# Projections of the second relational layer made inside the first, two accumulators for gathered blocks, and GIN's residual on TensorE

## The chip, the cores and the metric

One Trainium2 chip, one of its cores. Each time is the device time of one execution in microseconds (us); the number that counts is the median of the runs.

## The reference, cut to what matters

A graph of 3125 nodes with 128 features and 100000 edges, sorted by destination, goes through four parts, each followed by a residual and a layer norm: three GCN layers, one sum of neighbours, a GIN layer with two batch norms, and two relational layers. The change touches the end of the third part and the whole fourth:

```
h = relu(batchnorm(h @ W2 + b2))                      # end of GIN
x = layernorm(x + h)

def rgcn_layer(x, src, dst, etype, W, W_root, b, num_rels):      # 8 relations
    h = einsum('ni,rio->rno', x, W)
    msg = h[etype, src]
    seg = dst * num_rels + etype
    mean = segment_sum(msg, seg) / maximum(segment_sum(1, seg), 1)
    return mean.reshape(N, num_rels, do).sum(axis=1) + x @ W_root + b

h = relu(rgcn_layer(x, src, dst, edge_type, W1, root1, b1, 8))   # 128 -> 256
x = layernorm(x + rgcn_layer(h, src, dst, edge_type, W2, root2, b2, 8))   # 256 -> 128
```

## The kernel before, in words

The nodes are cut into 25 blocks of 128, and the blocks into chunks of four or three, `CH = ((0, 4), (4, 3), (7, 4), (11, 3), (14, 4), (18, 3), (21, 4))`. From the edge list the kernel builds count matrices in memory first: one over all edges (`adj`, `adj_t`) for the first three parts, and one for each relation (`rel`, 8-bit counts) for the destinations of blocks 0 to 13. The destinations of blocks 14 to 24 get no relation matrix; there the rows of the sources are gathered edge by edge. The dense part and the gathered part of a relational layer run side by side.

GIN ends with a loop over `CH` (L661 to L667): the transposed result `y2` is turned back by TensorE into a PSUM tile, DVE adds the residual to `xa`, and `normalise` (L118) makes the layer norm: statistics of each block on DVE, a square root on ACT, a reciprocal and the scaling of each block on DVE.

The relational layers hold float32 rows in several pieces, so that fast matmuls keep the precision. `split2` (L691) makes a pair of float32r pieces (the tile `hilo`). `store3` (L697) makes three bf16 pieces by copy on ACT, subtraction on DVE, copy on ACT, subtraction on DVE, with the tiles `t3` (shown as t) and `e3` (shown as e) of two buffers each, and stores them to a table in memory by a DMA on SP's queue: `xt_d` for layer 1's input, `ht_d` for layer 2's, one table of 3200 rows for each relation.

`relation` (L712) makes one product of a chunk of destinations with the rows of all 25 source blocks, for one relation. In each of five groups it loads 8-bit counts of five source blocks (`m8`, six buffers, on SP), casts them to float32r (`m`, three buffers; DVE for groups 0, 2, 4 at L728, ACT for 1 and 3 at L726), and multiplies with both pieces into the PSUM tile `acc` (L731, three buffers). After each group it advances `work` by a rate of 2.2 steps.

`work` is the generator `gathered` (L742). A step gathers 128 edges' rows from the table by an indirect DMA of GpSimd (`gx`, L765, twelve buffers), and adds them by three bf16 matmuls with a one-hot tile `oh` (made on DVE, L757) into `ga` (L773), a PSUM tile of 128 x 1024, one buffer, for one destination block and all relations. At the end of a block `put1` (L820) or `put2` (L893) evicts it.

In layer 1 the loop L827 takes the four dense chunks, for each the eight relations, with the means in `z` (L832); `linear1` (L796) then multiplies `z` by the eight matrices W1 and adds the root term, starting with the root term (L806), then L808, in float32, and ACT writes `hT` (L810), the transposed hidden rows. For the gathered chunks `put1` calls `linear1`. All of linear1's PSUM tiles are of the tag `mi`, two buffers.

Layer 2 begins with the root term `oT` (L872). `project` (L842) then makes h W2 for one relation after the other, for each block two float32 matmuls of 128 columns (L848), four or three blocks a PSUM tile, and each tile goes through `store3`. Relation 7 is made last, and its pieces are also split straight from PSUM, since layer 2 begins with it; the other relations' rows come back from memory by `fetch` (L854: load, two additions, split). The loop L906 takes for each relation the four dense chunks, scales (L913) and adds (L915); the gathers for layer 2 need the whole table. `finish` makes the last layer norm.

The order of instructions on each engine is fixed before the run by a scheduler: it takes the program's order as priority, and lets a later instruction go first where, by its own model of times, the earlier one is not ready. At run time each engine and each queue keeps to that order. The recording counts each float32 matmul as two instructions.

Of the kernel before, what the change touches and what calls it, by code (L numbers as in the profile page):

```python
# [21 lines left out]
P = 128  # L22
D = 128
# [22 lines left out]
def cols(m0, nb):  # L46
    return slice(m0 * P, (m0 + nb) * P)
# [25 lines left out]
def listed(ctx: ExitStack, tc: tile.TileContext, p: dict, out: bass.AP, bad):  # L73
# [43 lines left out]

    def normalise(y, v, nb):  # L118

        st = small.tile([P, 4, 6], F32, name="st")  # L120
        mv = small.tile([P, 4, 2], F32, name="mv")
        for i in range(nb):
            nc.vector.bn_stats(st[:, i, :], v[:, i, :])
            nc.vector.bn_aggr(mv[:, i, :], st[:, i, :])
        rs = small.tile([P, 4], F32, name="rs")
        nc.scalar.activation(rs[:, :nb], mv[:, :nb, 1], AF.Sqrt, bias=eps_ln, scale=1.0)
        nc.vector.reciprocal(rs[:, :nb], rs[:, :nb])
        for i in range(nb):
            nc.vector.tensor_scalar(
                y[:, i, :], v[:, i, :], mv[:, i, 0:1], rs[:, i : i + 1],  # L130
                op0=OP.subtract, op1=OP.mult,
            )
# [4 lines left out]
    def blocks(ap):  # L137
        return ap.rearrange("p (b c) -> p b c", c=P)

    with tc.tile_pool(name="f_bg", bufs=1) as bg, tc.tile_pool(  # L140
# [322 lines left out]
        with tc.tile_pool(name="f_nd", bufs=1) as nd:  # L463
# [209 lines left out]
    with tc.tile_pool(name="f_rel", bufs=1) as rp, tc.tile_pool(  # L673
# [17 lines left out]
        def split2(pieces, m0, nb, x):  # L691

            hi, lo = [t[:, m0 : m0 + nb, :] for t in pieces]
            nc.scalar.copy(hi, x)
            nc.vector.tensor_sub(lo, x, hi.bitcast(F32))  # L695

        def store3(table, row0, m0, nb, x):  # L697

            t = rp.tile([P, 4, 3, D], BF, name="t3", bufs=2)
            a, b, c = [t[:, :nb, i, :] for i in range(3)]  # L700
            e = rp.tile([P, 4, D], F32, name="e3", bufs=2)[:, :nb, :]
            nc.scalar.copy(a, x)  # L702
            nc.vector.tensor_sub(e, x, a)  # L703
            nc.scalar.copy(b, e)  # L704
            nc.vector.tensor_sub(c, e, b)  # L705
            r0 = row0 + m0 * P
            nc.sync.dma_start(table[r0 : r0 + nb * P].rearrange("(b p) c -> p b c", p=P),
                              t[:, :nb].rearrange("p b i c -> p b (i c)"))

        ahead = [0.0]  # L710

        def relation(r, m0, nb, pieces, work, rate):  # L712

            acc = psum.tile([P, 512], F32, name="acc", tag="acc", bufs=3)
            w = nb * P
            for g in range(5):
# [12 lines left out]
                for k in range(5):  # L729
                    for i, x in enumerate(pieces):  # L730
                        nc.tensor.matmul(  # L731
                            acc[:, :w], x[:, 5 * g + k, :],
                            m[:, k].rearrange("p b d -> p (b d)")[:, :w],
                            start=(g == 0 and k == 0 and i == 0), stop=(g == 4 and k == 4 and i == 1),
                        )
# [6 lines left out]
        def gathered(table, rows, put):  # L742


            for g in range(NG):
# [37 lines left out]
        with tc.tile_pool(name="f_z", bufs=1) as zp:  # L783
            w1 = zp.tile([P, R, O1], F32, name="w1")
            nc.scalar.dma_start(w1, p["L3_gnn_W1"].rearrange("r i o -> i r o"))
            root1 = zp.tile([P, O1], F32, name="root1")
            nc.scalar.dma_start(root1, p["L3_gnn_root1"])
# [5 lines left out]
            for m0, nb in CH:  # L793
                store3(xt_d, 0, m0, nb, x3[:, m0 : m0 + nb, :])

            def linear1(z, m0, nb):  # L796
# [40 lines left out]
        with tc.tile_pool(name="f_hr", bufs=1) as hp:  # L837
            wr = hp.tile([P, 2, R, D], F32, name="wr", tag="wr")
            for a in range(2):
                nc.scalar.dma_start(wr[:, a], p["L3_gnn_W2"][:, a * P : (a + 1) * P, :].rearrange("r i o -> i r o"))  # L840

            def project(r, pieces):  # L842

                for m0, nb in CH:
                    o = psum.tile([P, 512], F32, name="mi", tag="mi", bufs=2)
                    for i in range(nb):
                        for a in range(2):
                            nc.tensor.matmul(o[:, cols(i, 1)], hT[:, a, cols(m0 + i, 1)], wr[:, a, r, :],  # L848
                                             start=(a == 0), stop=(a == 1))
                    store3(ht_d, r * NP, m0, nb, blocks(o[:, : nb * P]))  # L850
                    if pieces is not None:
                        split2(pieces, m0, nb, blocks(o[:, : nb * P]))

            def fetch(r):  # L854
# [14 lines left out]
            for m0, nb in CH:  # L869
# [21 lines left out]
            def put2(b, wn, acc, inv):  # L891
                s = hp.tile([P, P * R], F32, name="sg", tag="wr")
                nc.vector.tensor_mul(s[:, : wn * R], acc, inv)  # L893
# [10 lines left out]
            ahead[0] = -14  # L904
            order = [R - 1] + list(range(R - 1))
            for n, r in enumerate(order):  # L906
                nxt = None
                for i, (m0, nb) in enumerate(DENSE):
# [6 lines left out]
                    nc.vector.tensor_add(oT[:, c], oT[:, c], s[:, :w])  # L915
                    if i == 0 and n + 1 < R:
                        nxt = fetch(order[n + 1])
                    if n == R - 1:
                        finish(m0, nb)
# [620 lines left out]
```

## Time and profile before

| | us |
|---|---|
| median of 3 runs | 2266.65 |
| lowest, highest | 2266.39, 2271.27 |
| the profiled execution, its own time | 2383.56 |
| its span, first to last instruction | 2381.7 |

In the profiled execution TensorE's mean granted clock is 0.919, and the engines are busy for these shares of the span: TensorE 84%, its weight loads 60%, VectorE 62%, ScalarE 33%, GpSimd 38%. They are means over stages with different limits, so the stages have to be looked at one by one. A group in the profile is named by its line, its engine, its operation and by the tile written and the tiles read (`out<-in`). PE is TensorE, PEld its weight loads, DVE VectorE, ACT ScalarE, POOL GpSimd, and SP the engine whose queue issues most DMAs; SPq and ACTq are the queues. A busy TensorE is not a TensorE at its peak, since matmuls overlap in their pipeline and their ends are modelled.

### The profile page before, as it was taken

The page shows a single profiled execution, that of the slowest core. Times are in us where ns is not written, and L with a number is a line of the kernel's source. Part 1 is how long each engine was busy: PE and PEld are TensorE (multiplying, and loading weights), DVE is VectorE, ACT ScalarE, POOL GpSimd, SP SyncE. Part 2 cuts the span into 40 slices and gives each one's busy share as a digit, 9 for nine tenths or more (in the row PEclk, how much of TensorE's full clock was granted, in tenths as well). Part 3 has the DMA queues.
Part 4 walks back from the last instruction along what each step waited for, and adds up shares of the span by engine and source line. Part 5 has one row for each costly group of instructions (what it writes and reads, how often), then busy time and mean ns, then how long its engine had stood idle before and what let it go on. Part 6 is the DMA issues. An engine that isn't in the chain of part 4 may idle for free. (4 is left out here: it accounts for less than half of the span.)

```text
span 2381.7 us, 33681 instructions
## 1 busy us (share of the span) xinstructions
PE 1990.4 (84%) x13076; PEld 1424.5 (60%) x13076; DVE 1473.2 (62%) x2403; ACT 789.9 (33%) x1027; POOL 896.3 (38%) x898
## 2 busy tenths in 40 slices
PE   2676679999999999578989999888776798898785
PEld 1454446666655555256676775775675676776674
DVE  5888879999984310656443562441445677786764
ACT  1676725545431100422221221221343332322320
POOL 3222021212110000036575563772003577776665
PEclk9777789999999999689989999998998999998997
DMA  3444477888886665256465663662545677777662
GB/s 89 180 181 180 185 185 240 286 280 269 277 278 189 198 171 152 91 150 183 133 167 142 167 185 92 172 180 62 164 136 164 174 232 205 221 229 207 167 195 76
DMA packets 381459, 430.71 MB, mean 181 GB/s; under 512 B 28747, under 2 KB 347117, under 8 KB 381288
## 3 DMA queue, kind: packets, MB, share of 16 engines
q1 hardware_dynamic: 311134, 276.49, 38.4%
q0 software_dynamic: 45920, 119.66, 16.5%
q10 hardware_dynamic: 24234, 32.31, 4.5%
q8 instruction: 104, 1.70, 0.3%
q14 instruction: 67, 0.55, 0.1%
HBM read 316.76 MB, written 111.58 MB: 180 GB/s over the span
## 5 line engine op out<-in xcount | busy, mean ns | idle before, releaser
L731 PE MATMUL acc<-m,hilo 128*128 128x384 f32 (+1 forms) x3200 | 774.2, 386 | 56.2 <-issue 39.2
L731 PEld LDWEIGHTS acc<-m,hilo 128*128 128x128 f32 x3200 | 584.0, 196 | 137.9 <-issue 60.1
L765 POOL DMA_INDIRECT gx<-xt_d,gsrc x355 | 361.8, 1019 | 573.4 <-DMA m<-rel 339.8
L531 PE MATMUL acc<-m,parts 128*128 128x512 bf16 (+1 forms) x2625 | 539.0, 357 | 15.0 <-issue 12.8
L728 DVE CAST m<-m 128x2560 fp32r<-128x2560 uint8 (+1 forms) x192 | 401.8, 2097 | 231.5 <-ACT m L726 64.9
L765 POOL DMA_INDIRECT gx<-ht_d,gsrc x355 | 387.2, 1091 | 346.6 <-issue 265.9
L726 ACT CAST m<-m 128x1920 fp32r<-128x1920 uint8 (+1 forms) x128 | 264.2, 2064 | 622.5 <-PE ga L773 188.8
L531 PEld LDWEIGHTS <-parts 128*128 128x128 bf16 x2625 | 255.2, 98 | 237.4 <-issue 17.7
L773 PE MATMUL ga<-oh,gx 128*128 128x192 bf16 (+1 forms) x2442 | 265.7, 248 | 107.1 <-DVE sg L893 25.7
L773 PEld LDWEIGHTS <-gx 128*128 128x128 bf16 x2442 | 180.8, 100 | 194.0 <-issue 139.4
L448 ACT CAST rb<-bld 128x800 uint16<-128x800 f32 x179 | 143.9, 828 | 129.8 <-PE bld L441 121.6
L757 DVE TENSOR_TENSOR oh<-iota,gkey 128x768 bf16<-128x768 bf16 (+1 forms) x188 | 99.2, 530 | 133.8 <-PE ga L773 75.5
L455 POOL DMA_DIRECT2D rel<-rb x112 | 64.3, 582 | 287.5 <-ACT rb L448 162.7
L848 PE MATMUL mi<-wr,hT 128*128 128x128 f32 x800 | 107.2, 294 | 34.9 <-DVE e L703 33.8
L848 PEld LDWEIGHTS mi<-wr,hT 128*128 128x128 f32 x800 | 100.4, 205 | 42.7 <-DVE e L703 40.0
L154 DVE TENSOR_TENSOR lo<-iota,kT 128x2048 bf16<-128x2048 bf16 x100 | 122.0, 1220 | 0.8 <-PE bld L264 0.8
L441 PE MATMUL bld<-rhq,rlo 128*128 128x200 bf16 x896 | 107.7, 252 | 1.8 <-DVE rb L450 1.1
L264 PE MATMUL bld<-hi,lo 128*128 128x50 bf16 x1600 | 74.3, 200 | 39.9 <-DVE hi L154 24.5
L441 PEld LDWEIGHTS <-rlo 128*128 128x128 bf16 x896 | 82.5, 98 | 36.7 <-issue 9.1
L154 DVE TENSOR_TENSOR rhq<-iota,kT 128x3200 bf16<-128x3200 bf16 x56 | 102.2, 1824 | 0.0
L264 PEld LDWEIGHTS <-lo 128*128 128x128 bf16 x1600 | 63.5, 107 | 64.3 <-DVE hi L154 27.3
L276 PE MATMUL mi<-identb,at 128*128 128x128 bf16 x625 | 66.3, 272 | 34.0 <-ACT at L266 20.4
(211 smaller groups left out, 1801.4 us busy)
## 6 DMA issues: line engine op xcount, KB each, us to landing
m<-rel SPq DMA_DIRECT2D x160, 320.0 KB
rel<-rb POOLq DMA_DIRECT2D x112, 400.0 KB
m<-adj SPq DMA_DIRECT2D x60, 640.0 KB
m<-rel SPq DMA_DIRECT2D x160, 240.0 KB
m<-adj_t SPq DMA_DIRECT2D x40, 640.0 KB
m<-adj SPq DMA_DIRECT2D x45, 480.0 KB
adj_t<-at SPq DMA_DIRECT2D x25, 800.0 KB
adj<-av SPq DMA_DIRECT2D x25, 800.0 KB
```

Source lines behind the costliest of these rows:

```text
L154: nc.vector.tensor_tensor(o, (iota2 if of is None else of)[:, None, :width, :].to_broadcast([P, PU // 2, width, 2]), k[:, :, None, :].to_b ...
L264: nc.tensor.matmul(pt[:, j, : 2 * NB], lo[:, j // 2, :, j % 2], hi[:, j // 2, :, j % 2], start=True, stop=True)
L441: nc.tensor.matmul(pt[:, k, : R * NB], lo[:, j // 2, :, j % 2], hq[:, j // 2, :, j % 2], start=True, stop=True)
L448: nc.scalar.copy(o, src)
L531: nc.tensor.matmul(o, x[:, k, :], m(k - k0), start=(k == 0 and i == 0), stop=last and more is None)
L726: nc.scalar.copy(v, src)
L728: nc.vector.tensor_copy(v, src)
L731: nc.tensor.matmul(acc[:, :w], x[:, 5 * g + k, :], m[:, k].rearrange("p b d -> p (b d)")[:, :w], start=(g == 0 and k == 0 and i == 0), sto ...
L757: nc.vector.tensor_tensor(oh[:, : nt // 2], iota2[:, None, : GW * R, :].to_broadcast([P, nt // 2, GW * R, 2]), gkey[:, g, t : t + nt].rear ...
L765: nc.gpsimd.indirect_dma_start(out=gx.rearrange("p i c -> p (i c)"), out_offset=None, in_=table[:], in_offset=bass.IndirectOffsetOnAxis(ap ...
L773: nc.tensor.matmul(acc[:, a:z], gx[:, i, :], oh[:, t % 4 // 2, a - c0 : z - c0, t % 2], start=(a // 512 not in seen), stop=(t == GT[g] - 1 ...
L848: nc.tensor.matmul(o[:, cols(i, 1)], hT[:, a, cols(m0 + i, 1)], wr[:, a, r, :], start=(a == 0), stop=(a == 1))
```

## The change

- The projections h W2 move into `linear1`: as soon as a chunk of `hT` is written, two PSUM tiles of 512 columns are made for each of its blocks, each with four relations side by side (two float32 matmuls of 512 columns instead of eight of 128), and each goes through `store3`. `W2` is loaded at the beginning of layer 1. Layer 2 takes the relations in order from 0, and all of them through `fetch`.
- In `linear1` the root term is the last of the nine matmuls and no longer the first.
- `ga` gets two buffers, `acc` two instead of three. The tile of `put2` (sg) gets its own place.
- The rows of the cast tile `m` are 520 elements apart and no longer 512.
- In GIN's last loop two float32 matmuls of each block, one with `y2` and one with the identity and `xa`, add the residual in PSUM, in the tag `bld`; the norm reads PSUM, and every second block of it is scaled by ACT.

```diff
+    def normalise(y, v, nb, shared=False):
...
+        if shared:
+            ng = small.tile([P, 4], F32, name="ng")
+            nc.vector.scalar_tensor_tensor(ng[:, :nb], mv[:, :nb, 0], -1.0, rs[:, :nb],
+                                           op0=OP.mult, op1=OP.mult)
         for i in range(nb):
+            if shared and i % 2 == 0:
+                nc.scalar.activation(y[:, i, :], v[:, i, :], AF.Identity, bias=ng[:, i : i + 1],
+                                     scale=rs[:, i : i + 1])
+                continue
             nc.vector.tensor_scalar(
...
             for m0, nb in CH:
-                t = psum.tile([P, 512], F32, name="mi", tag="mi", bufs=2)
+                t = psum.tile([P, 512], F32, name="bld", tag="bld", bufs=2)
                 for i in range(nb):
-                    nc.tensor.transpose(t[:, cols(i, 1)], y2[:, cols(m0 + i, 1)], ident)
-                xs = xa[:, m0 : m0 + nb, :]
-                nc.vector.tensor_add(xs, blocks(t[:, : nb * P]), xs)
-                normalise(xs, xs, nb)
+                    o = t[:, cols(i, 1)]
+                    nc.tensor.matmul(o, y2[:, cols(m0 + i, 1)], ident, start=True, stop=False)
+                    nc.tensor.matmul(o, ident, xa[:, m0 + i, :], start=False, stop=True)
+                normalise(xa[:, m0 : m0 + nb, :], blocks(t), nb, True)
...
-            acc = psum.tile([P, 512], F32, name="acc", tag="acc", bufs=3)
+            acc = psum.tile([P, 512], F32, name="acc", tag="acc", bufs=2)
...
-                m = rp.tile([P, 5, 4, P], F32R, name="m", bufs=3)
-                v = m[:, :, :nb, :]
+                m = rp.tile([P, 5, 4 * P + 8], F32R, name="m", bufs=3)
+                v = m[:, :, :w].rearrange("p k (b d) -> p k b d", d=P)
...
-                acc = psum.tile([P, P * R], F32, name="ga", tag="ga", bufs=1)
+                acc = psum.tile([P, P * R], F32, name="ga", tag="ga", bufs=2)
...
+            wr = zp.tile([P, 2, R, D], F32, name="wr")
+            for a in range(2):
+                nc.scalar.dma_start(wr[:, a], p["L3_gnn_W2"][:, a * P : (a + 1) * P, :].rearrange("r i o -> i r o"))
...
-                    nc.tensor.matmul(o[:, :w], root1[:, c], x3t[:, :w], start=True, stop=False)
                     for r in range(R):
                         nc.tensor.matmul(o[:, :w], w1[:, r, c], z[:, r, :w],
-                                         start=False, stop=(r == R - 1))
+                                         start=(r == 0), stop=False)
+                    nc.tensor.matmul(o[:, :w], root1[:, c], x3t[:, :w], start=False, stop=True)
...
+                for b in range(m0, m0 + nb):
+                    for r in range(0, R, 4):
+                        o = psum.tile([P, 512], F32, name="mi", tag="mi", bufs=2)
+                        for a in range(2):
+                            nc.tensor.matmul(o, hT[:, a, cols(b, 1)],
+                                             wr[:, a, r : r + 4, :].rearrange("p r c -> p (r c)"),
+                                             start=(a == 0), stop=(a == 1))
+                        store3(ht_d.rearrange("(r n) c -> n r c", r=R)[b * P : (b + 1) * P, r : r + 4],
+                               blocks(o))
...
-            def project(r, pieces):
...
-            hr = pair()
-            for r in range(R):
-                project(r, hr if r == R - 1 else None)
...
-            order = [R - 1] + list(range(R - 1))
-            for n, r in enumerate(order):
+            hr = fetch(0)
+            for r in range(R):
```

More of the change, by code (lines that the diff above doesn't have):

```diff
@@ L115, in listed @@
     gsrc = [const.tile([P, NG, GM], I32, name=f"gsrc{i}") for i in range(2)]
-    def normalise(y, v, nb):
+    def normalise(y, v, nb, shared=False):
         st = small.tile([P, 4, 6], F32, name="st")
@@ L695, in split2, with store3 @@
             nc.vector.tensor_sub(lo, x, hi.bitcast(F32))
-        def store3(table, row0, m0, nb, x):
+        def store3(rows, x):
+            n = x.shape[1]
             t = rp.tile([P, 4, 3, D], BF, name="t3", bufs=2)
-            a, b, c = [t[:, :nb, i, :] for i in range(3)]
-            e = rp.tile([P, 4, D], F32, name="e3", bufs=2)[:, :nb, :]
+            a, b, c = [t[:, :n, i, :] for i in range(3)]
+            e = rp.tile([P, 4, D], F32, name="e3", bufs=2)[:, :n, :]
             nc.scalar.copy(a, x)
@@ L705, in store3 @@
             nc.vector.tensor_sub(c, e, b)
-            r0 = row0 + m0 * P
-            nc.sync.dma_start(table[r0 : r0 + nb * P].rearrange("(b p) c -> p b c", p=P),
-                              t[:, :nb].rearrange("p b i c -> p b (i c)"))
+            nc.sync.dma_start(rows, t[:, :n].rearrange("p b i c -> p b (i c)"))
         ahead = [0.0]
         def relation(r, m0, nb, pieces, work, rate):
-            acc = psum.tile([P, 512], F32, name="acc", tag="acc", bufs=3)
+            acc = psum.tile([P, 512], F32, name="acc", tag="acc", bufs=2)
             w = nb * P
@@ L732, in relation @@
                             acc[:, :w], x[:, 5 * g + k, :],
-                            m[:, k].rearrange("p b d -> p (b d)")[:, :w],
+                            m[:, k, :w],
                             start=(g == 0 and k == 0 and i == 0), stop=(g == 4 and k == 4 and i == 1),
@@ L793, in listed @@
             for m0, nb in CH:
-                store3(xt_d, 0, m0, nb, x3[:, m0 : m0 + nb, :])
+                store3(xt_d[m0 * P : (m0 + nb) * P].rearrange("(b p) c -> p b c", p=P),
+                       x3[:, m0 : m0 + nb, :])
             def linear1(z, m0, nb):
@@ L837, in listed @@
         with tc.tile_pool(name="f_hr", bufs=1) as hp:
-            wr = hp.tile([P, 2, R, D], F32, name="wr", tag="wr")
-            for a in range(2):
-                nc.scalar.dma_start(wr[:, a], p["L3_gnn_W2"][:, a * P : (a + 1) * P, :].rearrange("r i o -> i r o"))
-            def project(r, pieces):
[L844 to L852, printed above, removed]
             def fetch(r):
@@ L891, in put2 @@
             def put2(b, wn, acc, inv):
-                s = hp.tile([P, P * R], F32, name="sg", tag="wr")
+                s = hp.tile([P, P * R], F32, name="sg", bufs=1)
                 nc.vector.tensor_mul(s[:, : wn * R], acc, inv)
@@ L915, in listed @@
                     nc.vector.tensor_add(oT[:, c], oT[:, c], s[:, :w])
-                    if i == 0 and n + 1 < R:
-                        nxt = fetch(order[n + 1])
-                    if n == R - 1:
+                    if i == 0 and r + 1 < R:
+                        nxt = fetch(r + 1)
+                    if r == R - 1:
                         finish(m0, nb)
```

## The prediction

> **What bounds the kernel now.** I first looked for where the edited lines run (the views of single lines): the first relational layer's products (L731, tile acc) run from 1022 us, its last linear1 (L808) ends at 1652, the projections (L848) lie between 1662 and 1811, and from 1818 the second layer runs alone. Cut at those points, the table of stages reads (us, then busy us of each engine, TensorE's clock, the DMA share, GB/s):
>
> ```profile
> core 0: us, PE busy (x) PEld busy (x) DVE busy (x) ACT busy (x) POOL busy (x), PEclk, DMA share, GB/s
> 955.00:1022.00 67.00, 36.09 (x114) 20.85 (x111) 45.80 (x133) 33.64 (x54) 0.00 (x0) 0.72 0.36 110
> 1022.00:1605.00 583.00, 512.66 (x2887) 400.75 (x2887) 270.92 (x227) 137.60 (x81) 343.40 (x336) 0.93 0.57 156
> 1605.00:1652.00 47.00, 38.05 (x155) 21.90 (x156) 6.94 (x11) 3.17 (x6) 18.42 (x20) 0.85 0.24 68
> 1652.00:1818.00 166.00, 129.22 (x877) 113.91 (x876) 81.84 (x129) 71.67 (x130) 0.00 (x0) 0.95 0.43 141
> 1818.00:2382.00 564.00, 459.16 (x2798) 374.62 (x2797) 383.15 (x467) 151.96 (x102) 387.16 (x355) 0.91 0.66 190
> ```
>
> Layer 1 is TensorE's: 513 of 583 us, DVE under half, ACT a quarter. Between the layers stand 166 us in which GpSimd does nothing and no engine is full. In layer 2 TensorE has 459 of 564 us, DVE 383. So the first question is what times the 166 us. The chain of waits inside them, then who waited there:
>
> ```profile
> by line: DMA ht_d<-t 32.0%; DVE e L703 11.9%; DVE t L705 11.1%; PE mi L848 11.0%; ACT t L702 9.2%; ACT t L704 8.9%; PE mi L872 6.5%; issue 4.7%; DVE hilo L695 2.2%; PE acc L731 2.0%; DVE m L728 0.7%; ACTq L702 0.5%; DVEq L705 0.0%
> ...
> DVE e L703 <- ACT t L702: 70.3, 36, 27.2
> ACT t L702 <- DMA ht_d<-t: 46.0, 33, 4.2
> ...
> PE mi L848 <- DVE e L703: 33.8, 28, 2.7
> ```
>
> Not the matmuls (11%) but the splitting chain store3 sets the pace: copy, subtract, copy, subtract, store, and the copy of the next-but-one chunk waits until the store has landed (32% of the chain), since t3 has two buffers. 56 stores leave between 1666.9 and 1815.9: 149/55 = 2.71 us each.
>
> TensorE's own waits, 1022 to 1605 and then 1818 to 2344 (total us, times, longest), show the single accumulator of the gathered blocks: at a block's end the next block's matmuls wait for the eviction.
>
> ```profile
> PE ga L773 <- DVE z L820: 24.0, 6, 6.8
> PE acc L731 <- issue: 19.2, 26, 2.2
> ...
> PE ga L773 <- DVE sg L893: 25.7, 6, 7.9
> ...
> PE acc L731 <- DVE m L728: 11.2, 5, 5.4
> ```
>
> Last, the casts of the 8-bit relation blocks on DVE by shape (count, busy us, mean ns):
>
> ```profile
> L728 DVE CAST m<-m 128x2560 fp32r<-128x2560 uint8 x96 | 269.7, 2813 | 98.8 <-remote 45.7 <-issue 22.2 <-PE ga L773 15.8
> L728 DVE CAST m<-m 128x1920 fp32r<-128x1920 uint8 x96 | 132.5, 1381 | 132.7 <-ACT m L726 57.8 <-PE ga L773 34.9 <-issue 22.3
> ```
>
> The four-block form moves a third more elements and takes twice as long: 1.10 ns an element against 0.72.
>
> [...]
>
> **The change, part by part** (in the profiled execution's time).
>
> *1. Projections leave the gap.* L872 moves 12,800 columns (16 of 512, 12 of 384) in 10.74 us of the chain: 0.84 ns a column and record. A new output, 512 columns with four records, costs 1.72 us of TensorE; 50 make 86 us. Before: 800 records of 128, 16 in 1.80 us, 90 us. Weight loads fall from 800 to 200. So TensorE's work hardly shrinks; what changes is what lies beside it. store3 runs 50 times on 512 columns, not 56 times on 384 to 512: DVE 50 x (0.691 + 0.691) = 69 us, ACT 50 x (0.584 + 0.619) = 60 us, SP 50 stores for 56. The splitting of relation 7's pieces straight from PSUM goes (7 split2), and fetch runs 8 times for 7: five more loads on SP, behind the last stores and ahead of m8 loads, and 5 x (0.82 x 3) = 12 us of DVE.
>
> What stays after the last linear1 (before 1652, call it T): its four blocks make 8 outputs, 8 x 2.75 = 22 us, the last store lands 2.5 later. Root2's 10.7 us of matmuls fit into the waits. fetch(0)'s first chunk needs load, two adds, cast, subtract, some 7 us, and if the new pool's space frees only with the last projection it starts at about T+21; four more at 2.5 to 3 us feed the first product, which ends near T+45 to T+55. Before, the first evicted product (L913) started at 1818.6, T+167. Gain **115 us**, ends 100 and 125.
>
> *2. They enter layer 1.* The other 42 outputs bring 42 x 1.72 = 72 us to an engine with 583 - 513 = 70 us idle, in which it waits in scattered pieces of some 1 to 7 us. Ready matmuls can fill some; matmul order is fixed, so others stay. I take a third filled, **+50 us**; ends +15 (nearly all filled) and +115 (42 x 2.75, the projection pace passed on whole). DVE then has 271 + 59 of some 630 us and ACT 138 + 50: neither binds. New waits: ACT's copy waits for a t3 store with L726 casts behind it, SP's store waits for L705 with the m8 loads behind it. Cover: six m8 buffers at 583/160 = 3.6 us a group, 22 us, just one burst of 8 outputs; three m tiles, 11 us.
>
> *3. Second ga accumulator, third acc gone.* The 24 and 26 us of waits can go. In layer 1 that is among the idle time counted above. In layer 2 something else is late next (the gather waits, 12 us there; the casts): I take -12 (0 to -25). The third acc only covers an eviction (0.69 us) beside a product of ten or more us: 0 (to +5).
>
> *4. The padded m tile.* [...]4/3 of 1.38 = 1.84; saved 0.97 to 1.08 us each, about 100 us of DVE, half in each layer. In layer 1 TensorE hides it: 0. In layer 2 L728 has 8.4% of the chain, 47 us; a third of that gone is -15 (0 to -35). If GpSimd's gathers grow in return by 0.1 us, 355 of them cost 35 us, against 53 us in layer 2 in which gathers wait for ga matmuls: 0.
>
> *5. GIN's residual.* Seven adds (0.66 or 0.52) and 14 of 25 scalings (0.28 in the batches of the timeline) leave DVE, 7 small products (0.2) come: -7 us; TensorE's records go from 25 to 100 of 0.11 us, 8 us, beside it. DVE sets this stretch: **-5** (-8 to +3; the tile is held until the scaling).
>
> *6. Early load of wr; root1 last.* Two more issues on ACT's queue behind w1; there the inv loads already took 5.13 us to issue and the next rs waited 5.53: +3 (0 to +10). root1 last removes a wait on x3t of a few us: within part 2.
>
> Sum: -115 + 50 - 12 - 15 - 5 + 3 = **-94 us** on the profiled execution's 2383.56. The median of the runs is 2266.65, 0.951 of it; scaled, -89: **2178 us**.
>
> **Rivals.** *A, as above*, chance 0.62: 2145 to 2215.
> *B, the overlap fails.* Layer 1 is full, so the projections keep their own pace: +115 for +50, or the scheduler leaves them to the end. Sum -29, 2239 us. For it: 88% busy TensorE, and stretches without any gap. Against: the old gap was latency, and in the same layer TensorE, ACT and DVE all have some idle time. 0.20.
> *C, everything fills.* +15, and layer 2 gains -50 by DVE and ga: -152, 2122 us. For it: DVE's casts and ga waits are most of what the trace names. Against: GpSimd needs 355 x (1.09 + 0.30) = 493 us for layer 2's gathers alone. 0.10.
> *D, slower: SP's queue.* Every store in layer 1 holds SP for its chain (0.58 + 0.69 + 0.62 + 0.69 = 2.6) and its buffer's landing (2.5), and the m8 loads behind it, so TensorE, come late by all of it: 42 x 5.1 = 214 for +50, sum +70, 2333 us. It decides when an output costs TensorE more than (94 + 50)/42 = 3.4 us. For it: the cover of 22 us is used up by one burst. Against: there are 583 us for 7 bursts, and in the stretches of layer 1 that I looked at (1022 to 1100, 1500 to 1560) the m8 loads on SP wait only for a cast or a one-hot to free a buffer. 0.08.
>
> **Numbers.** 2178, from A. The range 2110 to 2250 takes A and B, and C. Faster 0.87, same 0.04 (B's edge), slower 0.09. Within 0.2% (4.5 us) is about what the runs, 2266 to 2271, can't tell from no change.
>
> **What would show it.** The stretch from the last L808 to the first L913 is 45 to 60 us for 167; layer 1 up to there is 30 to 80 longer, TensorE above 90% in it; L728's 2560 form is 1.7 to 1.9 us; both ga rows of waits shrink. Wrong: L731 waiting in layer 1 for m8 loads or for ACT's casts behind t3 (D); most projection matmuls still in a row after T, or TensorE waiting in layer 1 for the first subtraction of store3 (B).

## The result, and the profile after

The changed kernel takes **2261.44 us**, the median of eight runs (2257.66 to 2263.13), and the kernel before, beside it, 2267.99 us (2265.13 to 2271.27): a ratio of 0.997, 95% interval 0.9959 to 0.9981. A gain of 6.5 us stands where 89 were forecast.

To read the numbers below one has to know that the chips were of two kinds: on one of them the kernel before takes 2263 to 2282 us, on three others 2364 to 2417, with the same order of instructions. By its times the comparison above ran on the quicker kind; the profile that the prediction used (2383.56 us) has the time of the slower kind. Every ratio is against the kernel before on the same chip, and traces are compared within a kind unless the text says otherwise. `before_three` is a profile of the unchanged kernel on a quicker chip (2274.9 us, span 2273.0); the profiled execution of the changed one took 2260.0 us, span 2258.2.

The table of stages, cut at the first load of the relation counts, the last linear1 product and the first scaling of layer 2 (the columns are those of the prediction's table). Before, on the quicker kind:

```profile
988.00:1594.00 606.00, 546.94 (x3101) 421.15 (x3101) 308.89 (x309) 158.08 (x111) 363.89 (x355) 0.95 0.61 168
1594.00:1761.00 167.00, 129.35 (x878) 113.09 (x876) 82.68 (x130) 71.97 (x131) 0.00 (x0) 0.96 0.43 140
1761.00:2273.00 512.00, 439.70 (x2796) 364.95 (x2796) 381.80 (x466) 151.59 (x102) 388.10 (x355) 0.93 0.74 209
```

After:

```profile
1004.00:1684.00 680.00, 623.21 (x3268) 449.96 (x3268) 305.24 (x356) 205.78 (x193) 393.58 (x355) 0.96 0.62 175
1684.00:1735.00 51.00, 43.73 (x143) 24.27 (x141) 30.98 (x41) 23.52 (x34) 15.19 (x13) 1.00 0.62 188
1735.00:2258.00 523.00, 447.59 (x2765) 363.66 (x2765) 338.23 (x467) 149.74 (x101) 397.72 (x343) 0.93 0.73 202
```

The stretch between the layers falls from 167 us to 51. But layer 1 starts 16 us later, is 74 us longer, and layer 2 is 11 us longer: 16 + 74 - 116 + 11 = -15, the difference of the spans (rounded to the cuts). In layer 1 TensorE's busy time (first pair of numbers) rises by 76 us; its idle time is 59 us before and 57 after. In layer 2 DVE (the third pair) has 44 us less to do, and GpSimd (the fifth pair) is busy for 10 us more, though 12 of its 355 gathers now lie ahead of the stage.

What is left between the layers, by its waits:

```profile
POOL gx L772 <- DMA ht_d<-t: 52.3, 1, 52.3
DVE e L712 <- ACT t L711: 22.6, 7, 17.7
...
PEld mi L828 <- DVE e L712: 8.2, 6, 2.7
...
ACT t L711 <- DMA ht_d<-t: 5.6, 6, 1.8
```

The splitting chain is the same as before, but only the eight outputs of the last chunk remain of it; the 46.0 us in which ACT waited for stores (47.8 in `before_three`) are 5.6. GpSimd starts layer 2's gathers as soon as the last store has landed, at 1715.6, 18 us ahead of the first scaling at 1733.9; before it started at 1761.7, one after it.

The waits of TensorE in layer 2 (1735 to 2258):

```profile
PE ga L780 <- DMA gx<-ht_d,gsrc: 57.7, 65, 2.9
PE acc L738 <- DVE m L735: 5.4, 2, 3.3
```

And the same before, on the quicker kind (1762 to 2273):

```profile
PE ga L773 <- DMA gx<-ht_d,gsrc: 41.5, 39, 7.7
PE acc L731 <- DVE m L728: 10.2, 6, 4.1
PE ga L773 <- DVE sg L893: 8.1, 5, 2.5
```

The wait for the eviction (sg) is gone, the wait for casts has halved, and the wait for gathered rows is 16 us longer. The waits that the prediction set out to remove, 24 and 26 us in its profile, were 5.8 (for z) and 8.1 us on the quicker kind.

The casts by shape, after, are as forecast: the four-block form takes 1.78 us for 2.81.

```profile
L735 DVE CAST m<-m 128x2560 fp32r<-128x2560 uint8 x96 | 170.6, 1778 | 83.7 <-PE acc L738 51.2 <-ACT m L733 16.5 <-issue 13.2
L735 DVE CAST m<-m 128x1920 fp32r<-128x1920 uint8 x96 | 131.9, 1374 | 77.6 <-PE acc L738 41.3 <-issue 29.7 <-ACT m L733 6.6
```

### The profile page after: what moved, and what is told of

The parts are those of the page before. It is cut to its first block, busy times and chain, and to the rows that moved or that the text cites. A ratio compares the mean times of both kernels' runs of the same rounds, so it can differ in the third digit from the quotient of the medians.

```text
span 2258.2 us, 32584 instructions
## 1 busy us (share of the span) xinstructions
PE 1955.4 (87%) x12551; PEld 1351.3 (60%) x12551; DVE 1376.9 (61%) x2385; ACT 791.5 (35%) x1027; POOL 954.5 (42%) x898
## 5 line engine op out<-in xcount | busy, mean ns | idle before, releaser
L738 PE MATMUL acc<-m,hilo 128*128 128x384 f32 (+1 forms) x3200 | 758.5, 383 | 12.0 <-DVE m L735 6.6
L772 POOL DMA_INDIRECT gx<-xt_d,gsrc x355 | 393.6, 1109 | 573.2 <-DMA m<-rel 357.2
L738 PEld LDWEIGHTS acc<-m,hilo 128*128 128x128 f32 x3200 | 577.6, 193 | 80.3 <-issue 8.9
L772 POOL DMA_INDIRECT gx<-ht_d,gsrc x355 | 412.9, 1163 | 167.0 <-issue 56.4
L735 DVE CAST m<-m 128x2560 fp32r<-128x2560 uint8 (+1 forms) x192 | 302.6, 1576 | 161.3 <-PE acc L738 92.5
L780 PE MATMUL ga<-oh,gx 128*128 128x192 bf16 (+1 forms) x2442 | 273.5, 246 | 98.8 <-DMA gx<-ht_d,gsrc 57.7
L780 PEld LDWEIGHTS <-gx 128*128 128x128 bf16 x2442 | 170.7, 99 | 206.9 <-DMA gx<-ht_d,gsrc 83.1
L712 DVE TENSOR_TENSOR e<-mi,t 128x512 f32<-128x512 f32 x50 | 34.3, 688 | 133.8 <-ACT t L711 133.8
L828 PE MATMUL mi<-wr,hT 128*128 128x512 f32 x200 | 93.9, 604 | 4.8 <-DVE e L712 4.7
L285 ACT ACTIVATE av<-mi 128x896 bf16<-128x896 bf16 (+1 forms) x100 | 82.8, 835 | 31.4 <-PE mi L284 30.1
```

Of the source, the lines that this page charges most:

```text
L735: nc.vector.tensor_copy(v, src)
L738: nc.tensor.matmul(acc[:, :w], x[:, 5 * g + k, :], m[:, k, :w], start=(g == 0 and k == 0 and i == 0), stop=(g == 4 and k == 4 and i == 1),)
L772: nc.gpsimd.indirect_dma_start(out=gx.rearrange("p i c -> p (i c)"), out_offset=None, in_=table[:], in_offset=bass.IndirectOffsetOnAxis(ap ...
L780: nc.tensor.matmul(acc[:, a:z], gx[:, i, :], oh[:, t % 4 // 2, a - c0 : z - c0, t % 2], start=(a // 512 not in seen), stop=(t == GT[g] - 1 ...
L828: nc.tensor.matmul(o, hT[:, a, cols(b, 1)], wr[:, a, r : r + 4, :].rearrange("p r c -> p (r c)"), start=(a == 0), stop=(a == 1))
```

## The experiments

All times are medians; the ratio is to the kernel before in the same comparison, with its 95% interval. S is the slower kind of chip, Q the quicker.

| kernel | chip | us | before | ratio |
|---|---|---|---|---|
| proj_only | S | 2330.39 | 2396.65 | 0.9713 (0.9672 to 0.9755) |
| pad_only | S | 2377.36 | 2396.65 | 0.9917 (0.9887 to 0.9948) |
| gin_only | S | 2415.48 | 2396.65 | 1.0081 (1.0048 to 1.0115) |
| after_again | S | 2314.23 | 2379.61 | 0.9732 (0.9684 to 0.9780) |
| no_gin | S | 2298.37 | 2379.61 | 0.9685 (0.9643 to 0.9727) |
| no_pad | S | 2322.48 | 2379.61 | 0.9769 (0.9732 to 0.9806) |
| ga_only | Q | 2264.16 | 2271.56 | 0.9964 (0.9954 to 0.9975) |
| no_ga | Q | 2262.63 | 2271.56 | 0.9963 (0.9952 to 0.9975) |
| half_gather | S | 2206.06 | 2382.71 | 0.9274 (0.9230 to 0.9319) |
| no_pad_2 | S | 2324.91 | 2382.71 | 0.9749 (0.9708 to 0.9790) |
| no_gin_2 | S | 2302.62 | 2382.71 | 0.9661 (0.9624 to 0.9699) |
| no_gin_no_pad | S | 2302.15 | 2382.71 | 0.9668 (0.9635 to 0.9702) |
| half_gather_no_pad | Q | 2189.61 | 2267.77 | 0.9647 (0.9621 to 0.9674) |
| no_pad_3 | Q | 2230.05 | 2267.77 | 0.9839 (0.9818 to 0.9860) |
| no_gin_no_pad_2 | Q | 2211.00 | 2267.77 | 0.9737 (0.9716 to 0.9757) |

### The parts one by one

First the kernel before itself, unedited, to have its profile on the chips of the experiments (2416.94, 2377.16 and 2274.9 us).

> The kernel before, unchanged, profiled once more. Its first profiled execution took 2383.56 us against 2268 in the median; the kernel after took 2260 profiled and 2261 in the median. Theory A: the first profile held an execution in which the stretch between the layers was the slow one; then a profile near 2268 shows the gap (last L808 to first L913) at 50 to 80 us instead of 167, and moving the projections gained nothing. Theory B: the gap is 160 to 170 us as in the first profile, and the two layers themselves are some 115 us shorter than in it, so the change lengthens the layers by about what it takes out of the gap. Everything ahead of 990 us as in the first profile in both.

> The kernel before, profiled on the same chip as the other runs of this call. If its time is near 2268, the stages tell where it is shorter than in the profile of 2383.56: theory A1, in the gap between the layers (50 to 100 us for 167); theory A2, inside the two layers, where TensorE waited for issue, for ga evictions and for casts (some 60 us less in each). If it is near 2397, the stages are those of the first profile.

> The kernel before once more, beside the others of this call. On two chips it took 2397 and 2380 us and the kernel after 2314, and TensorE paused there inside a group of ten products with nothing to wait for; where the kernel before took 2268 and the kernel after 2261, the kernel after showed hardly such a pause. If this chip is of the first kind: about 2385, stages as in the first profile. If of the second: about 2268, and the stages show which of them gives up the 115 us: A1, the gap between the layers; A2, the layers.

Measured: the stretch from the last linear1 product to the first scaling is 167 us in all three, so it was no accident of one execution. What is shorter on the quicker chip are the two layers, 605 and 512 us for 660 and 556 in before_two. Theory B of the first expectation and A2 of the others came true.

**proj_only**: of the change only the projections in `linear1`, the early W2, the root term last, `fetch` for all relations and the own place of sg.

```diff
+                for b in range(m0, m0 + nb):
+                    for r in range(0, R, 4):
...
-            for r in range(R):
-                project(r, hr if r == R - 1 else None)
+            hr = fetch(0)
```

> The kernel before with the projections (and what goes with them: early W2, root term last, fetch of relation 0) alone; norm, cast tile, ga and acc as before. By the forecast's parts: gap -115, layer 1 +50, early load +3: about 2206 us. Theory A: no gap to close, 86 us of matmuls in a full layer 1: slower, 2300 or more. Theory B: gap -115, layer 1 longer by the 86 us of matmuls that it takes in, and somewhat more where the single ga accumulator waits: 2235 to 2265.

Measured: 69 us of gain (0.0287 x 2396.65), a ratio of 0.971, where the forecast's parts came to 2206 of 2268, 0.973. From the last linear1 product at 1733.9 to the first scaling at 1784.8 there are 51 us. So the overlap works without any other part.

**pad_only** and **gin_only**: the one line of the cast tile with its views, or GIN's loop with its norm, put into the kernel before.

```diff
-                m = rp.tile([P, 5, 4, P], F32R, name="m", bufs=3)
+                m = rp.tile([P, 5, 4 * P + 8], F32R, name="m", bufs=3)
```

> The kernel before with rows of 520 instead of 512 in the cast tile, nothing else; the instructions of TensorE, GpSimd and SP are in the same order. By the forecast: L728's 2560 form from 2.81 to 1.75 us, 0 in layer 1, -15 in layer 2: 2253 us. Rival: [...]the gathers grow by 0.07 to 0.1 us (they grew from 1.02 and 1.09 to 1.11 and 1.16 us with the whole change), and where the gathers set the pace 355 x 0.07 = 25 us come on top: 2268 to 2290.

> The kernel before with GIN's residual on TensorE and the norm from PSUM, shared with ACT, alone. The forecast said -5 (2263 us). By the profile of the kernel after, in which the first m8 load stands 15 us later than before, it costs 15: 2283 us, with pairs of chunks 8.5 us apart, since the PSUM tile is held until the scaling and the next pair's matmuls wait for it.

Measured: in the kernel before, on the slower kind, the padding gains 20 us, near the 15 that were forecast, and GIN's part alone **costs** 19 us. On the quicker kind neither was run alone.

**ga_only**, and **no_ga**, which takes the same part back from the changed kernel:

```diff
-            acc = psum.tile([P, 512], F32, name="acc", tag="acc", bufs=3)
+            acc = psum.tile([P, 512], F32, name="acc", tag="acc", bufs=2)
...
-                acc = psum.tile([P, P * R], F32, name="ga", tag="ga", bufs=1)
+                acc = psum.tile([P, P * R], F32, name="ga", tag="ga", bufs=2)
```

> The kernel before with two buffers for ga and two instead of three for acc, nothing else. By the forecast: the waits for the evictions of ga (24 + 26 us in the first profile) go, and 12 us of them in layer 2 and some 15 in layer 1 come through: -20 to -30. Rival: the next late thing, a gather that has not landed, takes the place of each: -10 to 0.

> The kernel after with one buffer for ga and three for acc. By the forecast 12 to 30 us slower than the kernel after. Rival as for ga_only: 0 to 10 slower.

Measured: alone it gains 8 us; without it the changed kernel is at 0.9963 where it was at 0.997 with it. Both are what the rivals had. Within the change, on the quicker kind, the second accumulator is worth nothing that can be measured; on the slower kind this was not run.

### Parts taken back

**after_again** is the changed kernel, unedited, on a slower chip; **no_gin** has GIN's old loop and norm, **no_pad** rows of 512 in the cast tile. no_gin_2 and no_pad_2 are the same two again beside **no_gin_no_pad**, which has both.

```diff
-                m = rp.tile([P, 5, 4 * P + 8], F32R, name="m", bufs=3)
+                m = rp.tile([P, 5, 4 * P], F32R, name="m", bufs=3)
```

```diff
-                t = psum.tile([P, 512], F32, name="bld", tag="bld", bufs=2)
+                t = psum.tile([P, 512], F32, name="mi", tag="mi", bufs=2)
...
-                    nc.tensor.matmul(o, y2[:, cols(m0 + i, 1)], ident, start=True, stop=False)
-                    nc.tensor.matmul(o, ident, xa[:, m0 + i, :], start=False, stop=True)
-                normalise(xa[:, m0 : m0 + nb, :], blocks(t), nb, True)
+                    nc.tensor.transpose(t[:, cols(i, 1)], y2[:, cols(m0 + i, 1)], ident)
+                xs = xa[:, m0 : m0 + nb, :]
+                nc.vector.tensor_add(xs, blocks(t[:, : nb * P]), xs)
+                normalise(xs, xs, nb)
```

> The kernel after, unchanged, timed beside the kernel before on one chip. On the chip of the last call the kernel before took 2397 us where it had taken 2268 in the first comparison. Theory A (the chip or its condition slows what the kernel before waits for, and the kernel after has less of it): where the kernel before takes about 2397, the kernel after takes 2260 to 2310, a ratio of 0.94 to 0.965 as my forecast had it from a profile at 2384; where the kernel before takes 2268, the ratio is 0.997. Theory B (the first ratio holds on every chip): 0.997 in both cases, so 2390 beside 2397.

> The kernel after with GIN's last loop and the norm as before. gin_only cost 18.8 us on the kernel before; so -16 to -19 against the kernel after. If the later start of layer 1 is hidden by something else, 0.

> The kernel after with rows of 512 in the cast tile, order of TensorE, GpSimd and SP unchanged. pad_only gained 19 us on the kernel before. In the kernel after GpSimd's gathers follow one another with 0.30 us between (period 1.48 us) through layer 2, so its pace may be theirs: with the gathers back from 1.16 to about 1.09 us, the kernel without the padding is then 10 to 25 us faster than the kernel after. If the casts still set the pace: 15 to 20 us slower.

> The kernel after with rows of 512 in the cast tile, a second time. On a chip where TensorE pauses, it was 8 us slower than the kernel after. On one where it does not (kernel before near 2270), theory G says: gathers back to 1.09 us, 355 x 0.07 = 25 us shorter in layer 2, of which 10 to 25 us come through, so 2236 to 2251 beside 2261. Theory T: 0 to 10 us slower.

> The kernel after with GIN's last loop and the norm as before, a second time; 16 us faster on a chip with pauses. On one without: again 13 to 19 us faster, 2243 to 2248, since all of it stands ahead of layer 1 with nothing beside it.

> Both together: GIN's loop and the norm as before, and rows of 512. Theory G: the sum of both, 25 to 40 us faster than the kernel after, near 2225 where the kernel before takes 2270. Theory T: as no_gin_2, or up to 10 us slower than it.

Measured: on the slower kind the whole change is worth 65 us (2379.61 - 2314.23). Taking GIN's part back gains 16 us more, as expected. Taking the padding back loses 8 us in the first comparison (the intervals overlap), which neither of its two expectations had, and changes nothing in the second, once GIN's part is out as well (2302.62 against 2302.15): there theory T came true and G did not. The traces fit this. On the slower kind GpSimd's gathers of layer 2 don't follow one another closely without the padding: counting what goes beyond the usual 0.30 us between two of them, no_pad_2 has 37 pauses, 49 us together, and after_again 12, 18 us together.

Why GIN's part costs is seen in the timeline of the changed kernel, from the first product (start, us, engine, line):

```profile
975.66 0.49 PE L673 MATMUL bld<-ident,y 128*128 128x128 f32 x2 [4.01 <-ACT y L659]
...
979.13 0.49 DVE L123 BATCH_NORM_STATS2 st<-bld 128x6 f32<-128x128 f32 x2 [4.43 <-PE bld L674]
...
983.08 0.76 DVE L137 TENSOR_SCALAR xa<-bld,mv,rs 128x128 f32<-128x128 f32 x2 [0.31 <-ACT xa L134]
983.54 0.80 PE L673 MATMUL bld<-ident,y 128*128 128x128 f32 x2 [2.85 <-DVE xa L137]
...
987.36 0.50 DVE L123 BATCH_NORM_STATS2 st<-bld 128x6 f32<-128x128 f32 x2 [3.52 <-PE bld L674]
```

TensorE fills both bld tiles, at first with two records every 0.43 us; DVE's statistics wait for it (4.43, then 3.52 us); then TensorE waits for the last scaling to free a tile (2.85). The two take turns, some 8 us for each pair of chunks. The pace of the records goes with the granted clock: one every 0.21 us from 976.0 to 979.6 and from 983 to 990, where it is 0.53 and 0.52 in the mean, and one every 0.11 us in between, where it is 0.99. Up to the first load of counts DVE waits 13.1 us for bld and TensorE 8.6 for xa; before, the same loop had TensorE wait 4.0 us for DVE in all, as the addition already frees its PSUM tile.

### Halving the gathers of layer 2

**half_gather** leaves out every second gather of layer 2; the matmuls of such a step take the rows of the gather before, so half of the gathered rows are missing from its result.

```diff
-                    gx = rp.tile([P, 3, D], BF, name="gx", bufs=12)
-                    nc.gpsimd.indirect_dma_start(
...
+                    if t % 2 == 0 or table is xt_d:
+                        gx = rp.tile([P, 3, D], BF, name="gx", bufs=12)
+                        nc.gpsimd.indirect_dma_start(
```

> The kernel after, but in layer 2 only every second gather is made; the other step's matmuls use the rows of the gather before, so half of layer 2's gathered rows are left out and all of TensorE's, VectorE's and ScalarE's work stays. Theory G (GpSimd paces layer 2: 355 gathers x (1.16 + 0.30) = 519 us for a layer of 523): layer 2 falls to what TensorE needs, 430 to 480 us, the whole by 40 to 90 us. Theory T (TensorE paces it): less than 15 us faster.

Measured: 108 us less than the changed kernel on another slower chip (2206.06 for 2314.23), more than the 40 to 90 that were expected, with all matmuls and casts still there. Layer 2 goes from 543 us to 437 (1767.3 to 2203.9). TensorE now waits there for nothing of weight,

```profile
PE acc L738 <- DVE m L735: 7.0, 2, 3.6
```

and it is GpSimd that is held:

```profile
POOL gx L773 <- PE ga L781: 198.5, 146, 6.8
```

The test is not clean: TensorE's granted clock in layer 2 is 0.99, where after_again has 0.91, and its busy time there falls from 458 us to 415 with the same matmuls (458 x 0.91 = 417 and 415 x 0.99 = 411).

```profile
1768.00:2204.00 436.00, 415.37 (x2765) 353.93 (x2765) 333.98 (x468) 150.03 (x101) 212.96 (x166) 0.99 0.73 203
```

So some 43 of the 106 us may come from the clock; why it rose is not shown. The traces of the quicker kind say more. Before, the 355 gathers start from 1761.7 to 2256.8, 495 us, and 355 x (1.093 + 0.30) = 495: there is no slack between them. In the changed kernel they start from 1715.6 to 2242.2, 527 us, and 355 x (1.163 + 0.30) = 519. And the last runs below halve the gathers on one quicker chip without the padding: 2189.61 us for 2230.05, 40 less (clock in layer 2 0.97 for 0.94). So GpSimd's gathers set the pace of layer 2 in the changed kernel on the quicker kind, and this could have been read from a trace of that kind before the change. On the slower kind they have slack before: in before_two 40 pauses beyond the 0.30 us, 44 us together.

### On the quicker kind

The last three runs ask whether the padding costs where nothing else hides it. no_pad_3 is no_pad, no_gin_no_pad_2 is no_gin_no_pad, and half_gather_no_pad has both the halved gathers and rows of 512.

> The changed kernel with the cast tile's rows at 512. Theory G: where TensorE does not pause (before near 2270 us), gathers are 0.07 us shorter, and this kernel is 10 to 25 us faster than the changed kernel: 0.985 to 0.992 of before. Where it pauses (before near 2380), 0.972 to 0.978 again, no faster than the changed kernel. Rival T: on a chip near 2270 it is 0 to 10 us slower than the changed kernel, 0.997 to 1.001 of before.

> The changed kernel with GIN's residual on VectorE and the cast tile's rows at 512: projections and buffers alone. Where TensorE does not pause (before near 2270 us): the GIN part costs 16 us and, by theory G, the padding 10 to 25 us, so 0.978 to 0.986 of before. Where it pauses: 0.963 to 0.970 again. Rival T: near 2270 only the 16 us of GIN are won, less 0 to 10 us: 0.990 to 0.995.

> The changed kernel with every second gather of layer 2 left out (its matmuls take the rows of the gather before, so half of layer 2's gathered rows are not read) and with the cast tile's rows at 512 again. Theory G (GpSimd's gathers pace layer 2, the faster casts lengthen them): with half of the gathers gone GpSimd has room, so the padding now pays: this kernel takes 10 to 30 us more than the half-gather kernel with padding, which was 0.927 of before, so 0.932 to 0.940. Rival T (the casts matter nowhere in layer 2, TensorE paces): no difference from the half-gather kernel, 0.924 to 0.930.

Measured: no_pad_3 at 0.9839 lies just beyond the strong end of what theory G expected, 31 us under the changed kernel's 2261.44; the kernel before took 2267.77 us beside the one and 2267.99 beside the other. **In the changed kernel the padding costs 31 us on the quicker kind.** no_gin_no_pad_2 at 0.9737 goes beyond too: another 19 us, which are GIN's part. At 2211.0 us it is the best version that makes all gathers, 57 us under the kernel before and 50 under the changed one.

The gathers of layer 2 as groups (count, busy us, mean ns, then idle), before on the quicker kind,

```profile
L765 POOL DMA_INDIRECT gx<-ht_d,gsrc x355 | 388.1, 1093 | 294.5 <-issue 249.4 <-PE ga L773 22.6 <-DMA gx<-ht_d,gsrc 12.8
```

after,

```profile
L772 POOL DMA_INDIRECT gx<-ht_d,gsrc x355 | 412.9, 1163 | 167.0 <-issue 56.4 <-DMA ht_d<-t 52.3 <-PE ga L780 31.2
```

and with the rows of 512 (no_pad_3):

```profile
L772 POOL DMA_INDIRECT gx<-ht_d,gsrc x355 | 384.8, 1084 | 167.6 <-issue 57.0 <-PE mi L877 52.3 <-PE ga L780 34.6
```

A gather means 1163 ns with the padding and 1084 without: 355 x 0.079 = 28 us. The stages of no_pad_3 put it where it belongs:

```profile
1004.00:1680.00 676.00, 622.59 (x3265) 452.22 (x3266) 355.09 (x355) 205.77 (x193) 365.05 (x355) 0.96 0.62 176
1680.00:1731.00 51.00, 43.60 (x143) 24.32 (x141) 31.95 (x41) 23.25 (x33) 15.62 (x13) 1.00 0.61 188
1731.00:2226.00 495.00, 432.88 (x2765) 358.96 (x2765) 381.37 (x467) 149.76 (x101) 369.13 (x343) 0.94 0.76 213
```

Layer 2 is 495 us for 523, and layer 1 four shorter, though DVE has 43 and 50 us more to do. Layer 2 is then also 17 us shorter than before the change (512), about the time by which its gathers now start ahead of the first scaling.

Which gathers grow can be counted from the two traces, by the casts that a gather overlaps in time. Of layer 2's gathers those beside a cast of 2560 elements mean 983 ns without padding (137 gathers) and 1324 with it (84). Those beside a cast of 1920 elements, which runs at the quick rate in both, mean 1333 and 1362. The median of all is 947 and 948. So a gather that meets a quick cast takes some 0.35 us more, and the padding turned the other half of the casts quick: 84 x 0.34 = 29 us. (A long gather meets more casts than a short one, which could feign such a difference; but the median of those beside the slow casts of 2560 is 946, like that of all.)

half_gather_no_pad fell on a quicker chip and half_gather on a slower one, so the two ratios, for which its expectation was written, say nothing. Their layer 2 can be set side by side with care: 458 us without padding (1728.3 to 2186.0), 437 with it, though the latter's chip is of the slower kind. TensorE's waits without padding show a part of it:

```profile
PE acc L738 <- DVE m L735: 18.7, 10, 6.0
```

That is 18.7 us for 7.0. Once GpSimd has room, the padding may pay, as casts then are what TensorE waits for; with two chips, one profile of each and a granted clock of 0.97 against 0.99 this is not shown.

## Why the prediction was wrong

It forecast a gain of 94 us of 2383.56, scaled to 89, and a range of 2110 to 2250; the changed kernel stands at 2261. **Two steps had the wrong sign on the quicker kind.** Part 4, the padding, was to gain 15 us, with the longer gathers put at nothing; it costs 31. Part 5, GIN's residual, was to gain 5; it costs 19. The other parts were to gain 74 (70 scaled) and gain 57 (no_gin_no_pad_2). Together -57 + 31 + 19 = -7, where a gain of 6.5 us was measured. By stage, from the spans of one profile of each (slower kind: before_two, 2375.4, and after_again, 2313.9):

| step | forecast | slower kind | quicker kind |
|---|---|---|---|
| up to the first load of counts (part 5) | -5 | +16 | +16 |
| layer 1 to the last linear1 (parts 2 and 6) | +53 | +53 | +74 |
| from there to layer 2's first scaling (part 1) | -115 | -117 | -117 |
| layer 2 to the end (parts 3 and 4) | -27 | -13 | +12 |
| sum | -94 | -61 | -15 |

- **Part 1 was right** to 2 us, on both kinds of chip: the 167 us were the latency of the splitting chain, and eight outputs of it plus the first `fetch` remain. The landings of stores on that chain took 2.19 to 3.76 us in the prediction's trace; of what they consist no run shows.
- **Part 2**: +50 was right on the slower kind, where TensorE's busy time in layer 1 grew by 74 us and its idle time fell from 94 us to 73, so some 20 us were filled. It was too small on the quicker kind. There "I take a third filled" failed: TensorE's busy time grew by 76 us for the 42 outputs that came in (1.81 us each, the forecast had 1.72), and its idle time stayed at 59 and 57 us, so almost nothing was filled. What keeps the rest idle was not tested; 38 us of it are waits for gathered rows. Rival D didn't come: over both layers the casts wait 7.3 us for m8 loads. Rival B had the full layer right, but not its price: the projections cost TensorE's own time, not the 115 us of their old pace, and in layer 1 their matmuls wait 1.1 us for the subtraction and their weight loads 8.6. Part 6 was not measured by itself.
- **Part 3**: -12 rested on waits of 24 and 26 us, which are 5.8 and 8.1 on the quicker kind. In the changed kernel it is 0 there (no_ga); that GpSimd paces layer 2 whatever is freed behind it is the likely reason.
- **Part 4** failed in what it set against its gain. The duration was right (1.78 us, forecast 1.73 to 1.84, of which the upper figure is 4/3 of the three-block form's 1.38): the spacing of the rows alone makes 2812 ns (no_pad_3) 1778 (the changed kernel), or 1.10 ns an element 0.69. That the spacing would do this was the author's assumption; the trace of the kernel before shows the two rates alone. The price was right too: "If GpSimd's gathers grow in return by 0.1 us, 355 of them cost 35 us", measured 0.079 (no_pad_3 against the changed kernel) and 31 us. It was set to 0 against 53 us in which gathers wait for ga matmuls. On the quicker kind these waits are 22.6 us in 74 pieces of at most 0.3 us: no slack. On the slower kind, from which the prediction's trace came, the slack was there, and the padding alone gained 20. The prediction even had the number that decides, 355 x (1.09 + 0.30) = 493 us, and used it against rival C alone; put beside its own layer 2 it says how little a quicker DVE could bring. By what way a quick cast lengthens a gather (1324 ns in the mean beside quick casts of 2560, 983 beside slow ones) no run tells.
- **Part 5** had the wrong sign too. "TensorE's records go from 25 to 100 of 0.11 us, 8 us, beside it" failed twice: most of the records came every 0.21 us, as the granted clock was 0.52 to 0.53 for much of this loop, and they lay not beside DVE's work but in turn with it, since the PSUM tile is held until the scaling. The prediction named that and priced it at +3 at worst; it is +16 to the first load, and 16 to 23 us in the medians.
- **The scaling** hid the rest. That the profiled execution was 5% longer than the median was spread evenly over all steps. It sits nearly all in the two layers: the gap is 167 us on both kinds, layer 1 is 660 and 605, layer 2 556 and 512. What separates them is in part a TensorE that pauses inside a group of ten matmuls for nothing that the trace shows. On the slower kind the page of waits has rows for it (before_two, layer 1),

```profile
PE acc L731 <- issue: 11.7, 24, 1.1
```

while on the quicker kind (before_three) there is no such row from 1040 to 1594. The prediction showed such a row, 19.2 us, and read it as idle time that could be filled.

So the largest effect, the gap, was sized correctly, and on the quicker kind nearly all of it was given back: by 42 projections that cost TensorE their whole time, by GIN's taking of turns and by gathers that quicker casts lengthen. That the prediction is nearer on the slower kind, 65 us gained of 94, is in part because its trace came from there.

## What to carry to other kernels

For each stage, set count x (duration + gap) of each serial engine against the stage's length before pricing anything else: where the two agree, that engine paces the stage (here 519 us of gathers in a layer 2 of 523); speeding up another can't shorten the stage and may lengthen it (by 28 us, 495 to 523, when DVE's casts went from 2.81 to 1.78 us). An operation made quicker on one engine has to be priced on the other engines that work beside it (the gathers went from 1084 to 1163 ns). When the profiled execution and the median differ, find out in which stage the difference sits before scaling by it, and don't count idle time that only one of them has.

## What the runs showed of the hardware

- Two kinds of chips run the same instruction order 5% apart; of the four in the experiments three were of the slower kind and one of the quicker. Counting gaps between successive L731 (or L738) matmuls, the traces of the slower kind have some 30 to 65 of them, 12 to 30 us together, those of the quicker kind 4 to 8, at most 7.5 us. The granted clock is lower on the slower kind too, and TensorE is busy for longer with the same matmuls: in layer 1 of the kernel before 566 us at 0.92 (before_two) and 547 at 0.95 (before_three), in layer 2 460 at 0.91 and 440 at 0.93. An estimate from these figures: gaps (25 us) and longer busy time (39 us) make up some 65 of the 100 us. Where the gaps and the lower clock come from stays open. The traces of the slower kind also hold fewer semaphore records (18,147 to 20,936 for 28,561 to 31,559), so some of the gaps may be waits that were not recorded.
- An indirect gather of 128 rows on GpSimd takes 0.95 to 1.02 us in the mean beside a cast at 1.10 ns an element, and 1.26 to 1.47 beside one at 0.69 to 0.72, in layers 1 and 2 and on both kinds of chip; in the prediction's trace 0.97 and 1.30 in layer 1, 1.00 and 1.38 in layer 2, in the changed kernel 1.33 to 1.41 beside its casts, which are all quick.
- In GIN's last loop TensorE's records of 128 float32 columns come every 0.21 us where the granted clock is 0.52 to 0.53, and every 0.11 us where it is 0.99 (the changed kernel).
